# Two strips quantized in halves, a re-timed preparation queue and shared last combinations in a fused AdaLN/FFN kernel

## The chip, the cores and the metric

The kernel runs on one core of one Trainium2 chip. The metric is device time in microseconds (us) of one execution; the figure before is the median of three runs. Times inside an execution are counted from the start of the profiled span.

## What is computed

The reference, cut to what matters (`D = O = 2048`, 4096 tokens, everything f32):

```python
lora_delta = lora_B @ lora_A * 0.5
cb = codebook / max(abs(codebook))                  # 32 values, not sorted
normalized = (weight + lora_delta) / exp(scale_log) # groups of 128 columns
idx = searchsorted((cb[:-1] + cb[1:]) * 0.5, normalized, side='left')
quantized = cb[idx]
w = (quantized - normalized) + normalized
w_eff = w * exp(scale_log) + lora_delta
h = x @ w_eff.T
out = h @ W_base.T + b_base + 2 * mixed @ B_w.T     # mixed: router softmax over 8 rank-16 cores
return x + out
```

The kernel folds the two products: it computes `wc = W_base @ w_eff` (plus identity for the residual) once and then `x @ wc.T`.

## The kernel before

**Stage one: weights.** The weight matrix is handled in 16 strips of 128 columns (`[128, 16, 128]`, 2048 values for each partition). For each strip the quantizer walks the 31 thresholds in order. A level is one ACT instruction that writes a mask (`above`, L549, line of `raise_to`) and one DVE predicated copy that overwrites `a` with the level's value where the mask is set (L550). Four mask buffers let ACT run up to four levels ahead of DVE. The first levels of the *next* strip are made elsewhere: ACT makes the lowest level of each half in three passes (`scalar_level`: Relu L516, Sign L519, Identity L521; for level 3 of the first half the third pass is a Copy, L524), POOL makes two or three levels with a compare and an add each (`pool_levels`, L534 and L535) and adds level 3 (`last_level`, L539). So strips 1 to 5 have 27 full DVE levels, strips 6 to 15 have 27 and one half level.

After the last level, `straight_through` undoes and redoes the straight-through sum and multiplies by the scale (L572, L573, L574), on POOL in two halves, for the last strip on DVE in four quarters. Then TensorE multiplies the strip with four column blocks of `W_base`: `products(i, bs, c)` does quarter `c` of two blocks; the pair (2, 0) comes first, then (3, 1). Blocks 0 and 1 stay in SBUF, blocks 2 and 3 are streamed in 1 MB pieces (`wbp`) through three buffers. `low_rank` (L609) ends a block; `keep` copies it out of PSUM on ACT (L654) and stores it to `wc_dram` (L655). There are three PSUM buffers (`psum_m`) and five tiles for each strip (blocks 2, 0, the router part, 3, 1), so a new block waits for an older `keep`.

**Who sets the order.** Within this stage every engine runs its instructions in program order, and that order is written by hand: `behind(r, f, ...)` attaches a call to level `r`, and `quantize` emits those calls after the mask and copy of that level (I call this "hook r"). During strip `i` the hooks carry strip `i-1`'s products, strip `i+1`'s preparation (`delta` on TensorE, `scaled` on ACT, `normalize` on POOL, then the levels above) and, from strip 5 on, combinations of finished blocks.

**Combinations.** The second stage is a two-level Winograd-like product with seven by seven combined weights. `outer_w` and `inner_w` form these from `wc_dram` by adds and subtracts, and `put` stores them in `s_dram` (five DMAs for a pair of outer indices, three for a single one). For the first three groups this runs on POOL in the hooks (`made`). The last group (strips 12 to 15) can't be complete before the last strip is: outer index 1 needs strips 12 and 13 only (`first_fetch`, `first_make`, `first_put`); for blocks 0 and 2 the rest is `late_columns`, computed on DVE and put by DMAs issued from POOL; for blocks 1 and 3 it is done at the start of stage two (`last_fetch`, `last_outer`, `last_inner`, `last_put`). Tiles of stage two lie in memory that stage one used: `last_fetch(3)` fills a buffer that shares memory with `late`, so it waits until all of `late`'s puts have landed.

**Stage two.** 196 products `n` (L954), seven for each of 28 outer steps, with DVE, ACT and POOL combining the results; weights `s` are loaded from `s_dram` three products ahead on SP. DVE's part of the last combinations precedes its part of product 1 in DVE's program order (`u`, L1036).

Of the kernel before, what the change touches and what calls it, by code (L numbers as in the profile page):

```python
# [183 lines left out]
def adaln_ffn_kernel(  # L184
# [170 lines left out]
    def last_outer(b):  # L355
        outer_w(nc.vector, NK - 1, b)

    def last_inner(b, ms, z):
        inner_some(nc.vector, NK - 1, b, ms, z)

    def last_put(b, *sets):
        for ms in sets:
# [3 lines left out]
    with ExitStack() as sa:  # L366
# [145 lines left out]
        def scalar_level(i, f, r, part):  # L512
# [9 lines left out]
            elif part == 2:  # L522
                strips[i]["lx"] = mpool0.tile([P, NM // 2, P], F32, tag="lx", name=f"lx_{i}_{f}")
                nc.scalar.activation(strips[i]["lx"], sg, AF.Copy, scale=rise[:, r : r + 1])  # L524

        def half_step(i):
            return i - 1 in made

# [12 lines left out]
        def new_mask(i, r):  # L541
            return mpool.tile([P, F], F8, tag="above", name=f"above_{i}_{r}")

        def raise_to(i, r, above, f, n):
# [4 lines left out]
            nc.scalar.activation(above[:, c], q, AF.Relu, bias=neg_t[:, r : r + 1], scale=GAIN, saturate=False)  # L549
            nc.vector.copy_predicated(  # L550
                a, above[:, c].bitcast(U8), step[:, r : r + 1].to_broadcast([P, F // n])
            )

        def quantize(i, at):

            if half_step(i):
# [5 lines left out]
            assert not at, at  # L562

        def straight_through(i):
            last = i == NS - 1
            n = 4 if last else 2
            for h in range(n):
                m = ts(h, NM // n)
                w, a = strips[i]["w"][:, m, :], strips[i]["a"][:, m, :]
                sc = scale[:, strip[i], m].unsqueeze(2).to_broadcast([P, NM // n, P])  # L570
                v = nc.vector if last else nc.gpsimd
                v.tensor_tensor(a, a, w, ALU.subtract)  # L572
                v.tensor_tensor(a, a, w, ALU.add)  # L573
                v.tensor_tensor(a, a, sc, ALU.mult)  # L574
# [74 lines left out]

            nc.tensor.matmul(strips[i]["r"][:, P : P + RP], raw, stack, start=True, stop=True)  # L650

        def keep(i, b):
            out = spool.tile([P, 4, BC], F32, tag="out", name=f"out_{i}_{b}")
            nc.scalar.copy(out.rearrange("p q c -> p (q c)"), strips[i][b])  # L654
            (nc.scalar if i == NS - 1 else nc.sync).dma_start(wc_dram[i // 4][b][:, i % 4], out)  # L655

        def keep_router(i):
            nc.scalar.copy(rac[:, strip[i], :], strips[i]["r"][:, P : P + RP])
# [55 lines left out]
        def late_columns():  # L714

            t = big0.tile([P, NM, OQ], F32, tag="wb", name="late").rearrange("p m o -> p (m o)")
            for n, b in enumerate((0, 2)):
                f = t[:, 3584 * n : 3584 * n + 3584]
                columns(NK - 1, b, f[:, 0:2048], f[:, 2048:3584])
                fetch(NK - 1, b, range(3))  # L720
            for b in (0, 2):
                fetch(NK - 1, b, (3,))
            for b in (0, 2):
                if b == 0:
                    z = ypool.tile([P, 2048], F32, tag="up", name="late_z0")
                    z = (z[:, 0:1024], z[:, 1024:2048], t[:, 7168:8192])
                else:
                    more = ypool.tile([P, 1536], F32, tag="more", name="late_z1")
                    z = ypool.tile([P, 2048], F32, tag="up", name="late_z2")
                    z = (more[:, 0:1024], z[:, 0:1024], z[:, 1024:2048])  # L730
                last_outer(b)
                last_inner(b, (5, 6), z[0])
                last_inner(b, (2, 7), z[1])
                last_inner(b, (3,), z[2][:, 0:512])
                last_inner(b, (4,), z[2][:, 512:1024])
                last_put(b, (5, 6), (2, 7), (3,), (4,))


        made = {5: [(0, 0)], 6: [(0, 1)], 7: [(0, 2)], 8: [(0, 3)], 9: [(1, 0)], 10: [(1, 1)],
# [15 lines left out]
        for i in range(NS):  # L755
            at = {}

            def behind(r, f, *args):
                at.setdefault(r, []).append(lambda: f(*args))

            if i > 1:

                products(i - 2, (3, 1), NC - 1)
                route(i - 2, 0)
                behind(0, load_route, i - 2, 1)
                behind(2, keep, i - 2, 3)
                behind(3, keep, i - 2, 1)
            if i + 1 < NS:
                delta(i + 1, 0)
                if i > 0:  # L770
                    behind(1, load_w, i + 1, 2)
                behind(4, scaled, i + 1, 0)
                behind(4, normalize, i + 1, 0)
                behind(10, scaled, i + 1, 1)
                behind(10, normalize, i + 1, 1)
                for r, f, parts in ((0, 0, (11, 12, 13)), (NL - 1, 0, (14, 15, 18)), (0, 1, (19, 20, 21))):
                    for n, p in enumerate(parts):
                        behind(p, scalar_level, i + 1, f, r, n)
                behind(14, pool_levels, i + 1, 0)
                behind(19, last_level, i + 1, 0)  # L780
                behind(21, pool_levels, i + 1, 1)
            if i > 0:


                behind(9, load_route, i - 1, 0)
                if i == NS - 1:
                    behind(9, load_route, i - 1, 1)
                for c in range(2):
                    behind(2 + 3 * c, products, i - 1, (2, 0), c)
                if i + 1 < NS:  # L790
                    behind(7, delta, i + 1, 1)
                if i > 1:
                    behind(8, route, i - 2, 1)
                for c in range(2, NC):
                    behind(2 + 3 * c, products, i - 1, (2, 0), c)
# [5 lines left out]
                behind(19, router_sum, i - 1)  # L801
                behind(23, keep_router, i - 1)
                behind(18, router_parts, i - 1)
                if i + 2 < NS:
                    behind(20, load_la, i + 2)
            else:
                behind(3, nc.vector.reciprocal, rflat[:, NM:], flat[:, NM:])
                behind(7, delta, i + 1, 1)
                behind(22, lora_columns, 0)
                behind(24, lora_columns, 1)  # L810
                behind(25, lora_router)
            for n, (g, b) in enumerate(made.get(i, [])):
                step_of = (3, 5, 10, 13, 17, 23, 25) if len(made[i]) == 1 else (
                    (4, 6, 8, 9, 10, 12, 13) if n == 0 else (17, 19, 21, 22, 23, 24, 25)
                )
# [12 lines left out]

                behind((0, 14)[n], begin, g, b)
                r = step_of  # L830
                behind(r[0], outer_w, nc.gpsimd, g, b)
                behind(r[1], inner_pair, g, b, PAIRS[0])
                behind(r[1], inner_pair, g, b, PAIRS[1])
                behind(r[2], put, g, b, PAIRS[0])
                behind(r[3], put, g, b, PAIRS[1])
                behind(r[4], inner_pair, g, b, PAIRS[2])
                behind(r[4], inner_pair, g, b, PAIRS[3])
                behind(r[5], put, g, b, PAIRS[2])
                behind(r[6], put, g, b, PAIRS[3])
            quantize(i, at)  # L840
            straight_through(i)

        last = NS - 1
        products(last - 1, (3, 1), NC - 1)
# [10 lines left out]
        for bs in ((2, 0), (3, 1)):  # L855
            for c in range(NC):
                products(last, bs, c)
            if bs[0] == 2:
                multiply_router(last)
                router_parts(last)  # L860
            for b in bs:
                keep(last, b)
            if bs[0] == 2:
                router_sum(last)
                keep_router(last)
                late_columns()
        for h in range(2):
            route(last, h)
# [412 lines left out]
```

## Time and profile before

| | us |
|---|---|
| median of 3 runs | 2670.41 (2669.06 to 2674.28) |
| profiled execution | 2666.77 |
| its span | 2665.0 |
| TensorE busy | 2503.9 (94%) |
| DVE busy | 1549.0 (58%) |
| ACT busy | 1130.1 (42%) |
| POOL busy | 1367.2 (51%) |
| L550, DVE predicated copies | 1090.2 in 448 |
| L549, ACT masks | 872.4 in 448 |

The span falls into stage one (to about 1244.6, where the first product of stage two starts on TensorE) and stage two. Busy shares are means over both: DVE and ACT work nearly without a break in stage one and little in stage two, TensorE is nearly full in stage two. A row of the timeline gives the start, the length, the engine, the line, the operation with its tiles and shapes, how many instructions it merges, and in square brackets the idle time just before it with what ended it.

### The profile page before, as it was taken

To read this page: it belongs to the slowest core of one execution; us is meant where nothing else is said; L and a number is where in the kernel's file an instruction comes from. 1 tells how busy PE (TensorE), PEld (TensorE's weight loads), DVE (VectorE), ACT (ScalarE), POOL (GpSimd) and SP (SyncE) were. 2 spreads that over 40 slices of the span, in tenths; PEclk is the share of its full clock that TensorE was granted. 3 is DMA by queue.
4 is the path that set the end of the run, shared out by engine and by line. 5 is a ranking of instruction groups with operands and counts; after the bars stand their busy time and mean duration, and the time that the engine had idled before them with its cause. 6 is when DMAs were issued, how large, how long until landed. Compare 5 with 4: busy or idle time off the path is not lost.

```text
span 2665.0 us, 26423 instructions
## 1 busy us (share of the span) xinstructions
PE 2503.9 (94%) x10576; PEld 1704.1 (64%) x10576; DVE 1549.0 (58%) x990; ACT 1130.1 (42%) x796; POOL 1367.2 (51%) x783
## 2 busy tenths in 40 slices
PE   5499999999999999999999999999999999999999
PEld 2244444444444444345888888888888888888887
DVE  9999999999999999973433223242133332224221
ACT  7899999999999999930000000000000000000000
POOL 5777778889888888745313140042320323202224
PEclk9799999999999999999999999999999999999999
DMA  8255457776777777699844666536675455854554
GB/s 317 102 177 185 168 181 252 233 241 228 234 243 249 235 231 227 217 327 347 323 174 173 218 245 232 187 142 213 244 234 194 157 206 177 279 208 173 194 199 158
DMA packets 225979, 581.08 MB, mean 218 GB/s; under 512 B 20600, under 2 KB 121728, under 8 KB 182720
## 3 DMA queue, kind: packets, MB, share of 16 engines
q1 hardware_dynamic: 219296, 557.96, 61.1%
q0 software_dynamic: 4960, 14.95, 1.6%
q10 hardware_dynamic: 1600, 6.49, 0.7%
q8 instruction: 83, 1.36, 0.2%
q14 instruction: 40, 0.33, 0.0%
HBM read 477.62 MB, written 101.71 MB: 217 GB/s over the span
## 4 chain that ended last, share of the span: by engine, by line
PE 62%; ACT 17%; DVE 8%; POOL 7%; DMA 3%; issue 2%; SPq 0%; DVEq 0%; ACTq 0%; POOLq 0%
PE z L954 49%; ACT above L549 11%; PE m L621 10%; DVE a L550 7%; ACT sg L516 2%; ACT sg L519 2%; POOL a L572 1%; POOL a L573 1%; PE z L984 1%; ACT a L521 1%; POOL lv L534 1%; POOL a L574 1%; POOL a L535 1%; DMA xA<-in_xT 1%; DMA wc_dram<-out 1%
## 5 line engine op out<-in xcount | busy, mean ns | idle before, releaser
L550 DVE COPY_PREDICATED a<-above,step 128x2048 f32<-128x2048 uint8 (+1 forms) x448 | 1090.2, 2436 | 61.1 <-ACT above L549 19.3
L549 ACT ACTIVATE above<-w,neg_t 128x2048 fp8e5<-128x2048 f32 (+1 forms) x448 | 872.4, 1976 | 55.1 <-DVE a L550 44.5
L954 PE MATMUL z<-t,s 128*128 128x256 f32 x3584 | 791.4, 380 | 2.0 <-DVE u L1036 1.7
L954 PEld LDWEIGHTS z<-t,s 128*128 128x128 f32 x3584 | 677.5, 190 | 105.5 <-issue 13.2
L621 PE MATMUL m<-wbp,a 128*128 128x512 f32 x1024 | 502.1, 636 | 115.0 <-POOL a L574 101.0
L621 PE MATMUL m<-wb,a 128*128 128x512 f32 x1024 | 462.1, 594 | 4.4 <-ACT out L654 4.4
L621 PEld LDWEIGHTS m<-wbp,a 128*128 128x128 f32 x1024 | 202.6, 204 | 370.9 <-issue 239.7
L621 PEld LDWEIGHTS m<-wb,a 128*128 128x128 f32 x1024 | 194.5, 191 | 247.1 <-issue 242.4
L1034 ACT COPY m<-z 128x1024 f32<-128x1024 f32 x28 | 28.4, 1013 | 759.2 <-PE z L954 759.2
L1045 POOL TENSOR_TENSOR c<-u,m 128x1024 f32<-128x1024 f32 x16 | 50.1, 3130 | 443.8 <-DVE u L1042 422.4
L954 PE MATMUL z<-xA,s 128*128 128x256 f32 x1152 | 254.6, 379 | 0.0
L534 POOL TENSOR_SCALAR lv<-w,past,rise 128x1024 f32<-128x1024 f32 x65 | 245.9, 3783 | 3.7
L954 PEld LDWEIGHTS z<-xA,s 128*128 128x128 f32 x1152 | 218.8, 190 | 30.5 <-issue 0.8
L1045 POOL TENSOR_TENSOR M<-u,m 128x1024 f32<-128x1024 f32 x8 | 24.5, 3068 | 328.9 <-DVE u L1042 288.2
L954 PE MATMUL z<-xC,s 128*128 128x256 f32 x768 | 169.7, 379 | 0.0
L954 PE MATMUL z<-xB,s 128*128 128x256 f32 x768 | 169.7, 379 | 0.0
L535 POOL TENSOR_TENSOR a<-a,lv 128x1024 f32<-128x1024 f32 x65 | 154.3, 2374 | 27.1 <-ACT a L521 21.0
L1036 DVE TENSOR_TENSOR u<-z,m 128x1024 f32<-128x1024 f32 x28 | 34.3, 1224 | 218.5 <-issue 175.0
L1040 ACT COPY m<-z 128x1024 f32<-128x1024 f32 x28 | 28.3, 1011 | 308.8 <-PE z L954 308.8
L954 PEld LDWEIGHTS z<-xC,s 128*128 128x128 f32 x768 | 145.9, 190 | 19.8
L954 PEld LDWEIGHTS z<-xB,s 128*128 128x128 f32 x768 | 145.9, 190 | 19.8
L1042 DVE TENSOR_TENSOR u<-z,u 128x1024 f32<-128x1024 f32 x28 | 34.3, 1223 | 119.8 <-PE z L954 81.3
(213 smaller groups left out, 1958.0 us busy)
## 6 DMA issues: line engine op xcount, KB each, us to landing
s<-s_dram SPq DMA_DIRECT2D x196, 1024.0 KB, 4.9
wbp<-in_wbT SPq DMA_DIRECT2D x131, 1024.0 KB, 5.4
xs<-in_xT SPq DMA_DIRECT2D x64, 512.0 KB, 6.5
xA<-in_xT SPq DMA_DIRECT2D x24, 1024.0 KB, 9.4
s_dram<-z SPq DMA_DIRECT2D x84, 256.0 KB, 6.2
xB<-in_xT SPq DMA_DIRECT2D x16, 1024.0 KB, 10.4
outT<-M SPq DMA_DIRECT2D x16, 1024.0 KB, 12.5
w<-in_weight SPq DMA_DIRECT2D x30, 512.0 KB, 5.2
```

What stands on the lines that cost most here:

```text
L516: nc.scalar.activation(strips[i]["sg"], q, AF.Relu, bias=neg_t[:, r : r + 1], scale=GAIN)
L519: nc.scalar.activation(sg, sg, AF.Sign)
L534: v.tensor_scalar(lv, half(i, f, "w"), past[:, r : r + 1], rise[:, r : r + 1], ALU.is_gt, ALU.mult)
L535: v.tensor_tensor(a, a, lv, ALU.add)
L549: nc.scalar.activation(above[:, c], q, AF.Relu, bias=neg_t[:, r : r + 1], scale=GAIN, saturate=False)
L550: nc.vector.copy_predicated(a, above[:, c].bitcast(U8), step[:, r : r + 1].to_broadcast([P, F // n]))
L621: nc.tensor.matmul(ps, strips[i]["a"][:, CM * c + m, :], t[:, m, :], start=c == 0 and m == 0, stop=False)
L954: nc.tensor.matmul(z[:, c, :], s[:, k, ts(c, P)], rhs[:, k, :], start=not more and k == 0 and c % PER == 0, stop=k == NK - 1 and c % PER = ...
L1034: nc.scalar.copy(temp("m1", o), z["a"])
L1036: nc.vector.tensor_tensor(temp("u2", o), z["b"], state["m1", o], ALU.add)
L1042: nc.vector.tensor_tensor(temp("u3", o), z["d"], state["u2", o], ALU.add)
L1045: lambda d: nc.gpsimd.tensor_tensor(d, state["u3", o], state["m5", o], ALU.add),
```

## The change

- Strips 14 and 15 are quantized in two halves of the columns, one after the other: all levels of the first half (27 half levels), then all of the second (28). `straight_through` for the first half runs as soon as that half is done. A hook follows every second half level.
- For all other strips `straight_through` works on two quarters and then on the second half, where it worked on two halves. It stays on POOL but for the second half of the last strip, which is on DVE in two quarters.
- The second half of `delta`, the low-rank part of the next strip, moves from hook 7 (behind two quarters of the products) to hook 5 (behind one).
- `scaled`, `normalize`, the ACT passes, `pool_levels` and `last_level` get other hooks; the passes for the second half's lowest level come before those for level 3 of the first half.
- `keep` of blocks 2 and 0 moves from hooks 16 and 17 to hooks 14 and 15; `keep` of block 1 from 3 to 4; products from hooks 2, 5, 8, 11 to 4, 6, 8, 11.
- The combinations in the hooks get other places: two pairs early, the other two at hooks 24 and 25 with their puts at 25 and 26.
- For the last strip the two blocks of a pair are copied out of PSUM before anything is stored; the router's sum comes behind the first quarter of blocks 3 and 1.
- In `late_columns` both outer combinations come first on DVE; the inner ones of block 0 stay on DVE, those of block 2 go to POOL, between POOL's puts.

```diff
-        def straight_through(i):
-            last = i == NS - 1
-            n = 4 if last else 2
+        def halves(i, at):
+            n = 0
+            for f in range(2):
+                for k in range(T - NL + f):
+                    r = NL - f + k
+                    if n % 2 == 0:
+                        mask = new_mask(i, f"{f}{r}")
+                    raise_to(i, r, mask, f, 2, n % 2)
+                    n += 1
+                    if n % 2 == 0:
+                        for do in at.pop(n // 2 - 1, []):
+                            do()
+                if i == NS - 1 and f == 1:
+                    straight_through(i, f, nc.vector, 2)
+                else:
+                    straight_through(i, f, nc.gpsimd, 1 + f)
...
+            for f in range(2):
+                straight_through(i, f, nc.gpsimd, 2 - f)
...
-                behind(4, scaled, i + 1, 0)
-                behind(4, normalize, i + 1, 0)
-                behind(10, scaled, i + 1, 1)
-                behind(10, normalize, i + 1, 1)
-                for r, f, parts in ((0, 0, (11, 12, 13)), (NL - 1, 0, (14, 15, 18)), (0, 1, (19, 20, 21))):
+                behind(3, scaled, i + 1, 0)
+                behind(5, delta, i + 1, 1)
+                behind(7, scaled, i + 1, 1)
+                behind(5, normalize, i + 1, 0)
+                behind(9, normalize, i + 1, 1)
+                for r, f, parts in ((0, 0, (11, 12, 13)), (0, 1, (16, 17, 19)), (NL - 1, 0, (20, 21, 23))):
...
-                behind(16, keep, i - 1, 2)
-                behind(17, keep, i - 1, 0)
+                behind(14, keep, i - 1, 2)
+                behind(15, keep, i - 1, 0)
...
-                step_of = (3, 5, 10, 13, 17, 23, 25) if len(made[i]) == 1 else (
+                step_of = ((4, 8, 10), (4, 10, 12), (4, 24, 25), (4, 25, 26)) if len(made[i]) == 1 else (
...
+            for b in bs:
+                evacuate(last, b)
             if bs[0] == 2:
                 multiply_router(last)
                 router_parts(last)
             for b in bs:
-                keep(last, b)
+                store(last, b, nc.scalar)
...
+            last_inner(2, (5, 6), z[:, 0:1024], nc.gpsimd)
+            last_inner(2, (3,), z[:, 1024:1536], nc.gpsimd)
+            for b in (0, 2):
+                last_put(b, (5, 6))
+            last_put(2, (3,))
+            last_put(0, (2, 7), (3,), (4,))
+            z = ypool.tile([P, 2048], F32, tag="up", name="late_z2")
+            last_inner(2, (2, 7), z[:, 0:1024], nc.gpsimd)
+            last_inner(2, (4,), z[:, 1024:1536], nc.gpsimd)
+            last_put(2, (2, 7), (4,))
```

More of the change, by code (lines that the diff above doesn't have):

```diff
@@ L356, in last_outer, with last_inner @@
         outer_w(nc.vector, NK - 1, b)
-    def last_inner(b, ms, z):
-        inner_some(nc.vector, NK - 1, b, ms, z)
+    def last_inner(b, ms, z, v=nc.vector):
+        inner_some(v, NK - 1, b, ms, z)
     def last_put(b, *sets):
@@ L524, in scalar_level @@
                 nc.scalar.activation(strips[i]["lx"], sg, AF.Copy, scale=rise[:, r : r + 1])
+        HALVED = NS - 2
         def half_step(i):
@@ L542, in new_mask, with raise_to @@
             return mpool.tile([P, F], F8, tag="above", name=f"above_{i}_{r}")
-        def raise_to(i, r, above, f, n):
+        def raise_to(i, r, above, f, n, at=None):
             c = ts(f, F // n)
@@ L548, in raise_to @@
             a = strips[i]["a"].rearrange("p m i -> p (m i)")[:, c]
[L549 to L552, printed above, removed]
+            above = above[:, ts(f if at is None else at, F // n)]
+            nc.scalar.activation(above, q, AF.Relu, bias=neg_t[:, r : r + 1], scale=GAIN, saturate=False)
+            nc.vector.copy_predicated(a, above.bitcast(U8), step[:, r : r + 1].to_broadcast([P, F // n]))
         def quantize(i, at):
+            if i >= HALVED:
+                halves(i, at)
+                return
             if half_step(i):
@@ L561, in quantize, with straight_through @@
                     do()
-            assert not at, at
-        def straight_through(i):
-            last = i == NS - 1
-            n = 4 if last else 2
+            assert not at
+            for f in range(2):
[16 more added lines that the diff above has]
+                    straight_through(i, f, nc.gpsimd, 1 + f)
+            assert not at
+        def straight_through(i, f, v, n):
             for h in range(n):
-                m = ts(h, NM // n)
+                m = ts(n * f + h, NM // (2 * n))
                 w, a = strips[i]["w"][:, m, :], strips[i]["a"][:, m, :]
-                sc = scale[:, strip[i], m].unsqueeze(2).to_broadcast([P, NM // n, P])
-                v = nc.vector if last else nc.gpsimd
+                sc = scale[:, strip[i], m].unsqueeze(2).to_broadcast([P, NM // (2 * n), P])
                 v.tensor_tensor(a, a, w, ALU.subtract)
@@ L650, in router_sum, with evacuate, store, keep @@
             nc.tensor.matmul(strips[i]["r"][:, P : P + RP], raw, stack, start=True, stop=True)
-        def keep(i, b):
+        def evacuate(i, b):
             out = spool.tile([P, 4, BC], F32, tag="out", name=f"out_{i}_{b}")
             nc.scalar.copy(out.rearrange("p q c -> p (q c)"), strips[i][b])
-            (nc.scalar if i == NS - 1 else nc.sync).dma_start(wc_dram[i // 4][b][:, i % 4], out)
+            strips[i]["out", b] = out
+        def store(i, b, q=nc.sync):
+            q.dma_start(wc_dram[i // 4][b][:, i % 4], strips[i]["out", b])
+        def keep(i, b):
+            evacuate(i, b)
+            store(i, b)
         def keep_router(i):
@@ L723, in late_columns @@
             for b in (0, 2):
[L724 to L730, printed above, removed]
-                last_outer(b)
[L732 to L736, printed above, removed]
+                last_outer(b)
+            z = ypool.tile([P, 2048], F32, tag="up", name="late_z0")
+            last_inner(0, (5, 6), z[:, 0:1024])
+            last_inner(0, (2, 7), z[:, 1024:2048])
+            last_inner(0, (3,), t[:, 7168:7680])
+            last_inner(0, (4,), t[:, 7680:8192])
+            z = ypool.tile([P, 1536], F32, tag="more", name="late_z1")
+            last_inner(2, (5, 6), z[:, 0:1024], nc.gpsimd)
[8 more added lines that the diff above has]
+            last_put(2, (2, 7), (4,))
         made = {5: [(0, 0)], 6: [(0, 1)], 7: [(0, 2)], 8: [(0, 3)], 9: [(1, 0)], 10: [(1, 1)],
@@ L766, in adaln_ffn_kernel @@
                 behind(2, keep, i - 2, 3)
-                behind(3, keep, i - 2, 1)
+                behind(4, keep, i - 2, 1)
             if i + 1 < NS:
@@ L771, in adaln_ffn_kernel @@
                     behind(1, load_w, i + 1, 2)
-                behind(4, scaled, i + 1, 0)
-                behind(4, normalize, i + 1, 0)
-                behind(10, scaled, i + 1, 1)
-                behind(10, normalize, i + 1, 1)
-                for r, f, parts in ((0, 0, (11, 12, 13)), (NL - 1, 0, (14, 15, 18)), (0, 1, (19, 20, 21))):
+                behind(3, scaled, i + 1, 0)
[4 more added lines that the diff above has]
+                for r, f, parts in ((0, 0, (11, 12, 13)), (0, 1, (16, 17, 19)), (NL - 1, 0, (20, 21, 23))):
                     for n, p in enumerate(parts):
                         behind(p, scalar_level, i + 1, f, r, n)
-                behind(14, pool_levels, i + 1, 0)
-                behind(19, last_level, i + 1, 0)
-                behind(21, pool_levels, i + 1, 1)
+                behind(13, pool_levels, i + 1, 0)
+                behind(19, pool_levels, i + 1, 1)
+                behind(23, last_level, i + 1, 0)
             if i > 0:
@@ L788, in adaln_ffn_kernel @@
                 for c in range(2):
-                    behind(2 + 3 * c, products, i - 1, (2, 0), c)
-                if i + 1 < NS:
-                    behind(7, delta, i + 1, 1)
+                    behind((4, 6, 8, 11)[c], products, i - 1, (2, 0), c)
                 if i > 1:
@@ L794, in adaln_ffn_kernel @@
                 for c in range(2, NC):
-                    behind(2 + 3 * c, products, i - 1, (2, 0), c)
+                    behind((4, 6, 8, 11)[c], products, i - 1, (2, 0), c)
                 behind(13, multiply_router, i - 1)
-                behind(16, keep, i - 1, 2)
-                behind(17, keep, i - 1, 0)
+                behind(14, keep, i - 1, 2)
+                behind(15, keep, i - 1, 0)
                 for c in range(NC - 1):
                     behind((17, 20, 22)[c], products, i - 1, (3, 1), c)
-                behind(19, router_sum, i - 1)
-                behind(23, keep_router, i - 1)
+                behind(20, router_sum, i - 1)
+                behind(24, keep_router, i - 1)
                 behind(18, router_parts, i - 1)
@@ L807, in adaln_ffn_kernel @@
                 behind(3, nc.vector.reciprocal, rflat[:, NM:], flat[:, NM:])
-                behind(7, delta, i + 1, 1)
                 behind(22, lora_columns, 0)
@@ L812, in adaln_ffn_kernel @@
             for n, (g, b) in enumerate(made.get(i, [])):
[L813 to L814 removed]
+                step_of = ((4, 8, 10), (4, 10, 12), (4, 24, 25), (4, 25, 26)) if len(made[i]) == 1 else (
+                    ((4, 6, 8), (6, 6, 9), (10, 10, 12), (10, 10, 13)) if n == 0 else
+                    ((17, 19, 21), (19, 19, 22), (23, 23, 24), (23, 23, 25))
                 )
@@ L830, in adaln_ffn_kernel @@
                 r = step_of
[L831 to L839, printed above, removed]
+                behind(r[0][0], outer_w, nc.gpsimd, g, b)
+                for k, pair in enumerate(PAIRS):
+                    behind(r[k][1] if k else r[0][1], inner_pair, g, b, pair)
+                    behind(r[k][2], put, g, b, pair)
             quantize(i, at)
-            straight_through(i)
         last = NS - 1
@@ L857, in adaln_ffn_kernel @@
                 products(last, bs, c)
+                if bs[0] == 3 and c == 0:
+                    router_sum(last)
+                    keep_router(last)
+            for b in bs:
+                evacuate(last, b)
             if bs[0] == 2:
@@ L861, in adaln_ffn_kernel @@
             for b in bs:
-                keep(last, b)
+                store(last, b, nc.scalar)
             if bs[0] == 2:
-                router_sum(last)
-                keep_router(last)
                 late_columns()
```

## The prediction

> **What bounds the kernel now.** I read the page first, then the timeline of one strip engine by engine, then the chain of waits and the timeline where stage one hands over to stage two.
>
> ```profile
> PE 2503.9 (94%) x10576; PEld 1704.1 (64%) x10576; DVE 1549.0 (58%) x990; ACT 1130.1 (42%) x796; POOL 1367.2 (51%) x783
> ...
> L550 DVE COPY_PREDICATED a<-above,step 128x2048 f32<-128x2048 uint8 (+1 forms) x448 | 1090.2, 2436 | 61.1 <-ACT above L549 19.3
> L549 ACT ACTIVATE above<-w,neg_t 128x2048 fp8e5<-128x2048 f32 (+1 forms) x448 | 872.4, 1976 | 55.1 <-DVE a L550 44.5
> ```
>
> TensorE's 94% belongs to stage two. In stage one the bound is the row of predicated copies: 1090 us busy and 61 idle in about 1150. A full level takes DVE 2.47 us plus a gap of 0.10, so 2.57; a strip with 27 levels and a half one needs 70.8. The strips come every 71.6 (1029.84 to 1101.41). The difference is DVE waiting for a mask, 19.3 us in all, of which 49 ordinary gaps of 0.1 make 5. So all hook shuffling can win at most some 14 us.
>
> ```profile
> 1054.61 1.02 ACT L502 ACTIVATE a<-d 128x1024 f32<-128x1024 f32 x1 [3.34 <-PE d L410]
> ...
> 1088.78 70.49 DVE L550 COPY_PREDICATED a<-above,step 128x2048 f32<-128x2048 uint8 x28 [0.55 <-ACT above L549]
> ...
> 1106.50 1.90 POOL L574 TENSOR_TENSOR a<-a,scale 128x1024 f32<-128x1024 f32 x1
> ...
> 1108.45 6.34 PE L621 MATMUL m<-wbp,a 128*128 128x512 f32 x8 [5.60 <-POOL a L574]
> ```
>
> ACT loses its lead at hook 10, where it waits 3.34 us for the low-rank part; then five passes in a row (1.04, 0.94, 1.13 us) on top of a 1.90 us mask overrun DVE's 2.57. TensorE idles 5.6 us at each strip's start for POOL's first half and then runs slowly: 6.34 us for eight matmuls that otherwise take 3.60.
>
> ```profile
> L550 DVE COPY_PREDICATED a<-above,step 128x1024 f32<-128x1024 uint8 x14 | 18.3, 1317 | 0.2
> ```
>
> This is the half level: 1.33 us inside a strip, 1.43 with its gap.
>
> ```profile
> 1191.19 23.45 DMA xA<-in_xT
> ...
> 1215.74 5.40 PE L621 MATMUL m<-wb,a 128*128 128x512 f32 x8 [4.43 <-ACT out L654]
> ...
> 1226.21 2.62 DVE L320 TENSOR_TENSOR late<-late 128x512 f32<-128x512 f32 x4 [44.27 <-DMA late<-wc_dram]
> ...
> 1253.65 0.55 POOL L353 DMA_DIRECT2D s_dram<-late x1
> 1261.37 2.13 POOL L310 DMA_DIRECT2D last<-wc_dram x3 [7.16 <-DMA s_dram<-late]
> ...
> 1274.31 2.62 DVE L320 TENSOR_TENSOR last<-last 128x512 f32<-128x512 f32 x4 [9.12 <-DMA last<-wc_dram]
> ...
> 1288.53 7.17 PE L954 MATMUL z<-t,s 128*128 128x256 f32 x32 [1.71 <-DVE u L1036]
> ```
>
> This is the handover chain. The last strip's store sits behind xA's landing; then load, DVE combination, POOL's puts, the fetch for block 3 (only when all puts have landed), DVE again, and product 6 of TensorE waits 1.71 us for DVE. So what sets the end is not where stage two starts (1244.58) but when DVE gets through, and POOL is in that chain.
>
> **The change, part by part.** Times are from the start s of a strip, "before" from the trace.
>
> *Strips 1 to 13.* The first POOL quarter ends at 0.18 + 1.36 + 1.36 + 1.03 = 3.9 (512 columns take POOL 1.28 at L320, 1.36 with the gap; the multiply is taken as 1.03, somewhat over half of 1.90). Before, it was a half, at 7.0. TensorE thus starts 3.05 us earlier and ends blocks 2 and 0 at 37.65 where it was 40.7. `delta`'s second half now ends at about 14.7, so the 3.34 us stall shrinks to about 1 and is made up by hook 11. But the keep of block 2 stands at hook 14, two levels (5.14 us) earlier. ACT's greatest lead is three levels less a mask, 5.65, about 4.7 at hook 14: it arrives at 32.7 and waits 5 us for TensorE. The copy (0.47) and the next mask (2.0) end at 40.12, just when DVE wants level 15 (1.43 + 15 x 2.57 = 40.0). With the lead gone, the passes at 16, 17, 20 and 21 cost DVE 0.17 + 0.27 + 0.30 + 0.27; with 0.1 at level 15 that is 1.1, and about 0.1 of other gaps. Measured before: 0.8 on average in strips 6 to 13. So 0.4 more a strip, 3.4 in eight. In strips 1 to 5, which lack the half level, the same count gives 8.4 against 8.6. Together +3.2. One us of TensorE's arrival moves this by nearly one us a strip, so the term lies between -8 and +8.
> SP and POOL: the late puts at hooks 25 and 26 hold SP until POOL is through at about 69. Behind them stand a `wbp` piece that is needed 22 us into the next strip, the fetch for `up` (needed at 14) and the weight load (waits for POOL until 12.4 anyway): nothing if POOL keeps time, up to 2 us a strip if it doesn't. POOL's sum is 14.1 + 5.1 + 8.7 + 5.6 + 25 + 2.4 + 4.7 = 65.6 of 71.6.
>
> *Strips 14 and 15.* 55 half levels at 1.43 make 78.6 instead of 70.8: DVE ends 15.6 later in all. A rule of the Trainium skill speaks against this too: "VectorE: DVE Perf Modes", section on the TRN2 errata, says SBUF operations pay a fixed time per instruction, about 150 cycles as measured there. At 0.96 GHz that estimate is 0.156 us, so 27.5 more instructions would cost 4.3 a strip. The row says 2 x 1.43 - 2.57 = 0.29 each, 8 a strip, since each copy also waits for a mask; I take the row. What is it worth for TensorE? Products of 14 could start 5 us sooner, but block 0 needs the PSUM tile of the previous block 3, whose keep is at hook 2 of strip 15: ACT gets there at s14 + 79.9 (four mask buffers). The keep at hook 14 then holds blocks 3 and 1 until 112.8, the one behind the last mask holds strip 15's block 0 until 148.9, and quarter 2 needs DVE's end plus 2.5 = 159.5. Blocks 2 and 0 of strip 15 end at s14 + 175.3. Before: 1205.1 - 1029.84 = 175.3. Gain of halving: 0, with -4 to +6.
>
> *Handover.* Copying both blocks before storing removes TensorE's 4.43 + 0.35 us and the router's detour: stage two starts 5.5 earlier. xA's load comes at s14 + 161 as before (160.7; it waits for DVE's last subtract-add), but the x loads before it start about 4 us earlier, so fewer bytes are queued; I put the late combination's start t0 at s14 + 190 where it was 196.4 (bounds 188 and 196.4).
> Then POOL. Before, 32 puts of 0.72 ran from t0 + 1 to t0 + 28. Now POOL starts at t0 + 5.3 and has, besides, two pairs of 2.8 and two singles of 1.85, 9.3 us, all in one queue: last put at about t0 + 38.5. The landing (7.2 before, taken 6.5) gives the fetch at t0 + 45, where it was 35.2. Its data took 12.9 with stage two's loads around it; in the now quieter place I take 10. DVE resumes at t0 + 55, and needs 14.2 as before: t0 + 69.2 against 62.3. That is s14 + 259.2 against 258.7: +0.5, with -4 to +7. DVE's own saving, 5.4 us in `late_columns`, is worth nothing: it waits for the fetch.
> TensorE reaches product 6 at s14 + 251.4 and so idles 8 us. "TensorE: Matmul & The Clock Gate", Part 1, says that after an idle window of about 3.4 us the array runs at half rate for about as long, an estimate of 1.7 us lost. In the trace 4.5 to 5.6 us of idle cost 2.7 (6.34 against 3.60), the 1.71 us at product 6 nothing visible. I take 2.6; if the idle time is under 3 us it is 0.
>
> Sum: 3.2 + 0 + 0.5 + 2.6 = +6.3 on the profiled execution's 2666.77 (span 2665.0 and 1.8 around it), so 2673.1. The median of the runs shown is 3.6 above that execution: 2676.7, given as 2677. A measurement of this kernel can tell about 0.2%, 5.3 us, from no change.
>
> **Rivals.**
> *ACT keeps its lead (faster).* If TensorE ends blocks 2 and 0 only 1 us earlier than I count, all passes fit and each strip loses its 0.8: -8 in stage one. With t0 at s14 + 188 and a fetch of 8 us the handover adds -3.5 + 2.6. Sum -9, about 2662. For: the passes are spread better and the 3.34 us stall goes. Against: the keep at hook 14. Chance 0.20.
> *The handover doesn't come earlier (slower still).* The store waits for xA as before, t0 stays at s14 + 196.4, POOL's extra 7 us are paid in full, 265.6 against 258.7: +6.9 + 2.6 + 3.2 = +12.7, about 2683; to 2690 if DVE's longer halves also show. It decides from xA landing later than s14 + 183. Chance 0.18.
> *Terms cancel (no change).* No cold start and 0 in the strips leaves +0.5, about 2671. Chance 0.12.
> *My forecast*, 2670 to 2684 alone: 0.50, of which 0.12 lies within 0.2%.
> Slower 0.38 + 0.18 = 0.56, same 0.12 + 0.12 = 0.24, faster 0.20. For the range I leave out the lower half of the faster case and the top of the slower one: 2662 to 2688.
>
> **What would show it.** Right: ACT idle about 5 us at hook 14 for TensorE in each strip, with a small idle at hook 7; strips every 72.0; strips 14 and 15 of about 78.6 with half levels of 1.33; the fetch of block 3 about 45 us after the first late DVE combination; an idle of 4 to 12 us before product 6, then slow matmuls. Wrong: strips at 71.0 or less; product 6 without a wait; the start of stage two not earlier against strip 14's start; POOL idle gone at the end of strips, with TensorE starting later than 4 us.

## The result and the profile after

The changed kernel takes 2679.49 us (median of 7 runs, 2679.01 to 2684.2) where before takes 2670.41: ratio 1.0034, with a 95% interval of 1.0023 to 1.0045, so about 9 us slower. Its profiled execution took 2679.18, with a span of 2677.4. The profiled pair is 12.4 apart in span, more than the medians: before's profiled execution (2666.77) lies 3.6 below its median, after's 0.3 below.

From the page of after, engines and groups of instructions:

```profile
PE 2502.5 (93%) x10576; PEld 1703.2 (64%) x10576; DVE 1555.5 (58%) x1022; ACT 1136.6 (42%) x850; POOL 1391.9 (52%) x847
...
L554 DVE COPY_PREDICATED a<-above,step 128x2048 f32<-128x2048 uint8 (+1 forms) x502 | 1098.9, 2193 | 67.2 <-ACT above L553 20.6
L553 ACT ACTIVATE above<-w,neg_t 128x2048 fp8e5<-128x2048 f32 (+1 forms) x502 | 878.6, 1791 | 38.0 <-DVE a L554 28.3
```

TensorE's work is unchanged. In the DVE row the wait for masks hardly moved (20.6 where it was 19.3). In the ACT row the number behind the last bar tells more: ACT waits for DVE only when it is as far ahead as the four mask buffers allow. That wait fell from 44.5 to 28.3 us, so ACT was ahead less often. The half levels, in the groups by shape:

```profile
L554 DVE COPY_PREDICATED a<-above,step 128x1024 f32<-128x1024 uint8 x122 | 159.7, 1313 | 11.1
```

The timeline shows the loss in two places. The rows below give start, length, engine, line, operation, and in brackets the idle time before; first strip 10 in the middle of stage one, then the handover:

```profile
749.89 5.68 PE L646 MATMUL m<-wbp,a 128*128 128x512 f32 x8 [5.83 <-POOL a L599]
760.37 1.02 ACT L502 ACTIVATE a<-d 128x1024 f32<-128x1024 f32 x1 [0.43 <-PE d L410]
783.40 0.58 ACT L679 COPY out<-m 128x512 f32<-128x512 f32 x1 [4.65 <-PE m L634]
...
1222.98 2.62 DVE L320 TENSOR_TENSOR late<-late 128x512 f32<-128x512 f32 x4 [30.67 <-DMA late<-wc_dram]
1229.05 1.09 POOL L329 TENSOR_TENSOR late_z<-late 128x256 f32<-128x256 f32 x1 [10.60 <-DVE late L320]
1230.61 0.94 DVE L329 TENSOR_TENSOR late_z<-late 128x256 f32<-128x256 f32 x1
...
1256.98 0.72 POOL L329 TENSOR_TENSOR late_z<-late 128x256 f32<-128x256 f32 x1 [1.78 <-DMA s<-s_dram]
...
1266.71 0.55 POOL L353 DMA_DIRECT2D s_dram<-late  x1
1276.44 1.23 DVE L965 TENSOR_TENSOR t<-t,xA 128x1024 f32<-128x1024 f32 x1 [34.80 <-DMA s_dram<-late_z]
1277.14 2.15 POOL L310 DMA_DIRECT2D last<-wc_dram  x3 [9.88 <-DMA s_dram<-late]
1284.31 2.62 DVE L320 TENSOR_TENSOR last<-last 128x512 f32<-128x512 f32 x4 [2.64 <-DMA last<-wc_dram]
...
1298.51 9.60 PE L987 MATMUL z<-t,s 128*128 128x256 f32 x32 [15.79 <-DVE u L1069]
```

In stage one the stall for the low-rank part (3.1 to 3.5 us before, in strips 6 to 13) is 0.43 in strip 10, but ACT now stands 4.65 us at hook 14, where the `keep` of block 2 waits for TensorE. In the handover, DVE has its data 3.2 us earlier than before (1222.98 against 1226.21), POOL's last put is out 44.3 us after that, and the fetch for block 3 follows only when everything has landed. DVE, held by the same puts, stands idle for 34.80 us, and product 6 of TensorE waits 15.79 us instead of 1.71.

The span difference in three terms, with s14 the start of strip 14 and product 6 counted from it:

| | before | after | difference |
|---|---|---|---|
| s14 | 1029.84 | 1032.45 | +2.6 |
| product 6 starts, from s14 | 258.7 | 266.1 | +7.4 |
| product 6 lasts | 7.17 | 9.60 | +2.4 |
| sum | | | +12.4 |

### The profile page after: what moved, and what is told of

Its sections match the earlier page's. It is cut to its first block, busy times and chain, and to the rows that moved or that the text cites. A ratio compares the mean times of both kernels' runs of the same rounds, so it can differ in the third digit from the quotient of the medians.

```text
span 2677.4 us, 26622 instructions
## 1 busy us (share of the span) xinstructions
PE 2502.5 (93%) x10576; PEld 1703.2 (64%) x10576; DVE 1555.5 (58%) x1022; ACT 1136.6 (42%) x850; POOL 1391.9 (52%) x847
## 4 chain that ended last, share of the span: by engine, by line
PE 70%; ACT 13%; DVE 10%; POOL 3%; DMA 2%; issue 1%; SPq 0%; DVEq 0%; ACTq 0%; POOLq 0%
PE z L987 49%; PE m L646 17%; DVE a L554 9%; ACT above L553 9%; PE z L1017 1%; ACT sg L516 1%; ACT sg L519 1%; POOL a L597 1%; POOL a L598 1%; PE m L634 1%; PE d L410 1%; ACT a L521 1%; POOL a L599 1%; DMA wc_dram<-out 0%; PE acc L706 0%
## 5 line engine op out<-in xcount | busy, mean ns | idle before, releaser
L554 DVE COPY_PREDICATED a<-above,step 128x2048 f32<-128x2048 uint8 (+1 forms) x502 | 1098.9, 2193 | 67.2 <-ACT above L553 20.6
L553 ACT ACTIVATE above<-w,neg_t 128x2048 fp8e5<-128x2048 f32 (+1 forms) x502 | 878.6, 1791 | 38.0 <-DVE a L554 28.3
L1073 ACT COPY m<-z 128x1024 f32<-128x1024 f32 x28 | 28.3, 1011 | 308.5 <-PE z L987 308.5
```

The lines of the kernel that those rows point to most:

```text
L553: nc.scalar.activation(above, q, AF.Relu, bias=neg_t[:, r : r + 1], scale=GAIN, saturate=False)
L554: nc.vector.copy_predicated(a, above.bitcast(U8), step[:, r : r + 1].to_broadcast([P, F // n]))
L1073: nc.scalar.copy(temp("m5", o), z["c"])
```

## The experiments

My theory after the result: the loss is the new `late_columns`, above all POOL's longer queue, and the strips hide a gain that the `keep` at hook 14 takes back. The rivals: the loss comes from the halves of strips 14 and 15, or from the earlier passes in the strips. Ratios are to the kernel before, in runs beside it on the same chip, with 95% intervals.

### 1. The change with the former `late_columns`

```diff
-            last_inner(2, (5, 6), z[:, 0:1024], nc.gpsimd)
-            last_inner(2, (3,), z[:, 1024:1536], nc.gpsimd)
...
+                last_inner(b, (5, 6), z[0])
+                last_inner(b, (2, 7), z[1])
+                last_inner(b, (3,), z[2][:, 0:512])
+                last_inner(b, (4,), z[2][:, 512:1024])
+                last_put(b, (5, 6), (2, 7), (3,), (4,))
```

> The changed kernel with one part undone: late_columns is the former one (all combinations on DVE, block by block, puts as before). My theory (POOL's queue in the handover sets product 6): POOL's last put of `late` at about 28 us after the first late combination instead of 44, the fetch for block 3 at 35 instead of 54, product 6 of stage two within 4 us of its natural place, no slow matmuls; the time falls by 12 to 17 us against the changed kernel, to 2662 to 2668, below the kernel before. Rival (the handover wait comes from loads and memory, not from POOL's queue): product 6 still waits 8 us or more, and the time stays within 5 us of the changed kernel.

2671.14 us, ratio 0.9998 (0.9990 to 1.0007): no change against before, 8.4 less than after. The direction is as expected, the size is short of it. From its timeline:

```profile
1267.29 2.12 POOL L310 DMA_DIRECT2D last<-wc_dram  x3 [5.53 <-DMA s_dram<-late]
1278.26 7.07 PE L982 MATMUL z<-xA,s 128*128 128x256 f32 x32
1292.68 3.78 PE L982 MATMUL z<-t,s 128*128 128x256 f32 x8 [7.35 <-DVE u L1064]
```

The fetch comes 39.0 us after the first late combination (1228.32) where after has 54.2. But product 6 still waits 7.35 and starts slowly (its 32 matmuls take 9.93), where under 4 and no slow matmuls were expected. TensorE reaches it early: the earlier start of stage two has turned into a wait. Here `late` also came later than in after (s14 + 194.2 against 190.5), which took part of the gain.

### 2. Before, with the new `late_columns` alone

The same edit the other way round, on the kernel before.

> The kernel before with only the shared late_columns put in. My theory: it costs here what it costs in the changed kernel or a little more, since stage two starts later here: product 6 waits 13 to 16 us instead of 1.7 and starts slowly (2.4 us): +13 to +17 us, 2683 to 2688. Rival (the sharing is harmless by itself and hurts only with the earlier stage two): +0 to +4 us.

2682.98, ratio 1.0042 (1.0027 to 1.0057): 10.7 slower, somewhat less than expected. Its timeline:

```profile
1266.73 0.55 POOL L353 DMA_DIRECT2D s_dram<-late  x1
1276.34 2.16 POOL L310 DMA_DIRECT2D last<-wc_dram  x3 [9.07 <-DMA s_dram<-late]
...
1302.04 9.62 PE L959 MATMUL z<-t,s 128*128 128x256 f32 x32 [12.63 <-DVE u L1041]
```

With nothing else changed, the fetch moves from 35.2 to 48.3 us after the first late combination, and product 6 pays 12.63 and a slow start. Taken out (run 1) or put in (run 2), this edit is worth 8 to 11 us: the whole loss.

### 3. Run 1, with `keep` of blocks 2 and 0 back at hooks 16 and 17

```diff
-                behind(14, keep, i - 1, 2)
-                behind(15, keep, i - 1, 0)
+                behind(16, keep, i - 1, 2)
+                behind(17, keep, i - 1, 0)
```

> As x1_late_before, and the keeps of blocks 2 and 0 put back from hooks 14 and 15 to 16 and 17, nothing else. My theory (ACT loses its lead by waiting 4.65 us for TensorE at hook 14): the wait shrinks to under 1 us, ACT keeps a lead of 3 us or more, DVE's idle times go, strips 6 to 13 come every 70.9 to 71.1 us instead of 71.7 and strips 3 to 5 every 69.7 to 70.2 instead of 71.8; strip 14 starts 10 to 14 us earlier and the time falls by as much against x1_late_before. Rival (POOL, which has 3 us of slack, or TensorE sets the strips next): strips fall by 0.3 us or less each, the time by under 4 us.

2658.3, ratio 0.9948 (0.9934 to 0.9963): 12.8 less than run 1, as expected. ACT in strip 10:

```profile
748.33 1.02 ACT L502 ACTIVATE a<-d 128x1024 f32<-128x1024 f32 x1 [1.87 <-PE d L410]
...
771.36 0.59 ACT L679 COPY out<-m 128x512 f32<-128x512 f32 x1 [0.52 <-PE m L634]
```

And its row of masks:

```profile
L553 ACT ACTIVATE above<-w,neg_t 128x2048 fp8e5<-128x2048 f32 (+1 forms) x502 | 882.7, 1790 | 71.7 <-DVE a L554 60.4
```

The `keep` waits 0.52 instead of 4.65, and ACT is held back by DVE for 60.4 us where it was 28.3: it keeps its lead. Between the copies of strips 1 to 13 DVE idles 38.0 us, in run 1 55.0; the 359 ordinary gaps of 0.1 make 36 of both. Strips 6 to 13 come every 70.9 to 71.3, and strip 14 starts 16.9 us earlier than in run 1 (10 to 14 were expected).

### 4. Run 1 without the halves

```diff
-        HALVED = NS - 2
+        HALVED = NS
```

The last strip's second half of `straight_through` goes to DVE as in the change.

> As x1_late_before, but strips 14 and 15 are quantized in whole levels again, the last strip's straight-through sum on DVE in four quarters. My theory (halving is worth nothing: blocks 2 and 0 of the last strip end 174 to 175 us after strip 14's start either way): within 3 us of x1_late_before; strips 14 and 15 of 70.8 us instead of 77.6. Rival 1 (halving lets TensorE start earlier): slower by 4 to 8 us. Rival 2 (halving's 13.6 us of longer DVE work shows): faster by 4 us or more.

2671.52, ratio 1.0001 (0.9992 to 1.0010): the same as run 1. Strips 14 and 15 take 71.5 and 71.2 instead of 77.6 each, and yet blocks 2 and 0 of the last strip end at s14 + 175.3, against 177.2 in run 1 and 174.4 in after. Ends of DVE's levels that are over 12 us apart give ends within 2 us on TensorE.

### 5. After, with block 2's combinations on DVE but in the new order

```diff
-            last_inner(2, (5, 6), z[:, 0:1024], nc.gpsimd)
-            last_inner(2, (3,), z[:, 1024:1536], nc.gpsimd)
+            last_inner(2, (5, 6), z[:, 0:1024])
+            last_inner(2, (3,), z[:, 1024:1536])
...
-            last_inner(2, (2, 7), z[:, 0:1024], nc.gpsimd)
-            last_inner(2, (4,), z[:, 1024:1536], nc.gpsimd)
+            last_inner(2, (2, 7), z[:, 0:1024])
+            last_inner(2, (4,), z[:, 1024:1536])
```

> The changed kernel, block 2's inner combinations on DVE again, but in the new order of late_columns (both outer ones first, the puts of outer index 2, 7 and 4 of block 2 last). It separates POOL's arithmetic from the order. My theory (arithmetic in POOL's put queue, and POOL and DVE slowing each other while both combine): last put of `late` at about 34 us after the first late combination instead of 44, product 6 waits 6 to 9 us instead of 15.8; time 2669 to 2674, about that of x1_late_before. Rival (the order alone does it, since the single buffer for the last two combinations is refilled only after a landing): last put still at 40 us or later, time within 3 us of the changed kernel.

2677.76, ratio 1.0023 (1.0015 to 1.0031). Missed: the time, 1.7 us under after, is the one that the rival gave. In the trace the last put does come sooner, 36.9 us after the first combination against 44.3 (the rival had 40 or more), but a new wait took its place. The 15 runs spread from 2672.04 to 2683.92, and the profiled one, 2674.01, is among the lowest. Its timeline:

```profile
1252.14 0.42 DVE L329 TENSOR_TENSOR late_z<-late 128x256 f32<-128x256 f32 x1 [13.94 <-DMA s_dram<-late]
...
1257.20 8.06 PE L987 MATMUL z<-t,s 128*128 128x256 f32 x29 [10.48 <-issue]
```

DVE must wait 13.94 us for the buffer of block 2's later combinations, which is free only when block 0's puts from it have landed, and what makes product 1's input (`t`, L965) stands behind that in DVE's program order. Product 1 waits 10.48, product 6 no longer. Against run 1 the last put is 3.5 us later for the order of the puts; POOL's arithmetic added the other 7.4. So the order and POOL's arithmetic can be told apart in the traces; by the time, the order alone costs nearly as much as both.

### 6. Run 3 without the halves

> As x3_keep16, and strips 14 and 15 in whole levels as in x4_no_halves. My theory (halving is worth nothing to TensorE and costs DVE 13.6 us that only just hide): blocks 2 and 0 of the last strip end 175 us after strip 14's start instead of 179, product 6 comes 0 to 4 us earlier, time 2654 to 2659. Rival (halving gains once stage one runs faster): slower than x3_keep16 by 4 us or more.

2653.93, ratio 0.9932 (0.9917 to 0.9947): the fastest kernel here, 17.8 us under before and 25.6 under after. Run 3's interval overlaps, so it is not resolved whether leaving out the halves brings something; a gain from having them shows in neither pair (1 and 4, 3 and 6). This kernel differs from run 4 by the two `keep` calls alone, and takes 17.6 us less.

### 7. and 9. Before, with `delta`'s second half alone moved

```diff
-                    behind(7, delta, i + 1, 1)
+                    behind(3, delta, i + 1, 1)
```

> The kernel before with one edit: the second half of delta stands at hook 3, behind one quarter of the products, instead of hook 7, behind two. My theory (the 3.34 us stall of ACT at hook 10 was what cost the strips of the kernel before): no stall at hook 10, ACT waits about 2 us for TensorE at hook 16 with lead to spare; strips 6 to 13 every 70.9 to 71.1 us instead of 71.7, strips 3 to 5 about 70.5; the time falls by 7 to 10 us, to 2661 to 2665. Rival (the passes in a row cost it, not the stall): strips fall by 0.3 us or less, the time by under 4 us.

2730.5, ratio 1.0213. At hook 3 the second half's low-rank part is made before ACT has read the first half's (hook 4), and there is one PSUM buffer for both, so the edit changes part of the computation and its waits: the time says nothing on the question. Run 9 asks it with hook 4 (`behind(4, delta, i + 1, 1)`).

> The kernel before with one edit: the second half of delta at hook 4 instead of 7, still behind the first half's scaled, on TensorE behind one quarter of the products instead of two. My theory (ACT's 3.34 us stall at hook 10 was what cost the strips of the kernel before): no stall at hook 10, ACT waits about 2 us for TensorE at hook 16 with lead to spare; strips 6 to 13 every 70.9 to 71.3 us instead of 71.7, strips 3 to 5 about 70.5 instead of 71.5; the time falls by 7 to 10 us, to 2662 to 2665. Rival (the passes in a row cost it, not the stall): strips fall by 0.3 us or less, the time by under 4 us.

2658.67, ratio 0.9952 (0.9937 to 0.9967): 12.9 faster for one number, more than the 7 to 10 expected. Between the profiled executions it is 8.0; the rest is before's low profiled execution. Strip 10, first the second half's row in before, then three rows of this run, where the wait of 3.48 is gone:

```profile
768.23 1.02 ACT L502 ACTIVATE a<-d 128x1024 f32<-128x1024 f32 x1 [3.48 <-PE d L410]
...
744.62 1.02 ACT L502 ACTIVATE a<-d 128x1024 f32<-128x1024 f32 x1
759.16 1.00 ACT L502 ACTIVATE a<-d 128x1024 f32<-128x1024 f32 x1
778.31 0.58 ACT L654 COPY out<-m 128x512 f32<-128x512 f32 x1 [1.68 <-PE m L609]
```

s14 falls from 1029.84 to 1022.21, which is nearly the whole difference of the pair; product 6 waits 1.70 as in before. The first quarter that lets TensorE start earlier isn't needed for this.

### 8. Run 3, with block 2's 16 puts issued by ACT

```diff
-                last_put(b, (5, 6), (2, 7), (3,), (4,))
+                if b == 0:
+                    last_put(b, (5, 6), (2, 7), (3,), (4,))
...
+                for ms in ((5, 6), (2, 7), (3,), (4,)):
+                    put(NK - 1, 2, ms, nc.scalar)
```

> As x3_keep16, with block 2's sixteen puts of late_columns issued from ACT's DMA queue behind the last stores instead of from POOL's. My theory (POOL's queue of 32 puts at 0.72 us each is what the fetch of block 3 waits for): the puts are all issued 25 us after the first late combination instead of 31, the fetch goes out at 31 to 33 instead of 36.7, product 6 waits under 3 us instead of 7.4 and does not start slowly; 5 to 9 us less than x3_keep16, 2649 to 2653. Rival (landing, not issuing, or ACT's own work behind the puts sets it): within 3 us of x3_keep16.

2664.76, ratio 0.9973 (0.9962 to 0.9985), 6.5 slower than run 3, so that theory and rival both missed. In its timeline (ACTq is ACT's issue of DMAs):

```profile
1230.08 1.37 ACTq L351 DMA_DIRECT2D s_dram<-late  x1
...
1244.99 1.07 ACT L902 COPY accs<-acc 128x512 f32<-128x512 f32 x2 [17.33 <-DMA s_dram<-late_z]
1246.12 6.11 PE L986 MATMUL z<-t,s 128*128 128x256 f32 x17 [10.60 <-ACT accs L902]
```

A put holds ACT for up to 1.37 us, the copies behind them come 17 us late, and product 1 waits 10.60. The fetch for block 3 is no earlier: 39.5 us after the first late combination (36.7 in run 3). POOL's half of the puts is over after 16.9, but ACT begins its half only at 13.7 and ends it at 30.6, no sooner than POOL ended all 32 in run 3 (30.7). The run therefore doesn't show what puts issued earlier would be worth.

### 10. Before, with only "copy both blocks, then store" and the router's sum moved

```diff
+            for b in bs:
+                evacuate(last, b)
...
-                keep(last, b)
+                store(last, b, nc.scalar)
```

> The kernel before with one part of the change: the last strip's two blocks are copied out of PSUM before either is stored, and the router's sum comes a quarter later. My theory (product 6 of stage two waits for the handover chain, not for TensorE): TensorE's 4.43 us idle goes and stage two starts 4 to 6 us earlier, but the first late combination and the fetch of block 3 stay within 2 us of their places, product 6 waits 5 to 8 us instead of 1.7 and starts slowly; time within -2 to +3 us of before. Rival (stage two's start sets the end): faster by 4 to 6 us.

2671.57, ratio 1.0001 (0.9992 to 1.0009). From its timeline:

```profile
1239.17 6.09 PE L964 MATMUL z<-xA,s 128*128 128x256 f32 x27
...
1289.93 10.07 PE L964 MATMUL z<-t,s 128*128 128x256 f32 x32 [3.38 <-DVE u L1046]
```

Stage two starts 5.4 us before that of the kernel before (1244.58), and `late` comes no earlier (s14 + 197.1 against 196.4), so TensorE waits longer: 3.76 at product 1 and 3.38 at product 6 (5 to 8 expected there). The gain is lost whole. The fetch for block 3 was expected to keep its place and didn't: it comes 40.2 us after the first late combination, 35.2 in before. SP's loads for stage two go out about 7 us earlier, and POOL idles 9.3 us between the first and the last of its 32 puts where it idled 4.3.

### 11. After, with only the two `keep` calls at hooks 16 and 17

The edit of run 3, on after.

> The changed kernel with only the keeps of blocks 2 and 0 back at hooks 16 and 17. My theory: stage one gains what it gained in x3_keep16 (strip 14 about 15 us earlier), the handover costs what it cost in the changed kernel; time 12 to 15 us below the changed kernel, 2665 to 2668, so this one hook decides the sign of the whole change. Rival (the handover eats the gain): within 5 us of the changed kernel.

2667.83, ratio 0.9985 (0.9978 to 0.9991), 11.7 less than after: two numbers turn the change from slower to faster than before. s14 is 1016.57 where it was 1032.45. Product 6 still waits 16.11 us for DVE:

```profile
1286.42 9.06 PE L987 MATMUL z<-t,s 128*128 128x256 f32 x32 [16.11 <-DVE u L1069]
```

### 12. Run 6, with block 0's 16 puts issued by SP

```diff
-                last_put(b, (5, 6), (2, 7), (3,), (4,))
+                for ms in ((5, 6), (2, 7), (3,), (4,)):
+                    put(NK - 1, b, ms, nc.sync if b == 0 else nc.gpsimd)
```

> As x6_keep16_no_halves, with block 0's sixteen puts of late_columns issued from SP's queue, ahead of the first three loads of s, and only block 2's from POOL's. My theory (the fetch of block 3 waits for POOL's 32 puts): POOL's last put of `late` at 22 to 24 us after the first late combination instead of 28.5, the fetch at 29 to 32 instead of 36, product 6 is ready 4 to 7 us earlier; but the first loads of s are issued about 10 us later, so stage two starts 3 to 5 us later; together 0 to 4 us faster than x6_keep16_no_halves, 2650 to 2654. Rival (SP's queue held back costs more than POOL's saves): slower by 2 us or more.

2663.4, ratio 0.9969 (0.9954 to 0.9983), 9.5 slower than run 6, as the rival said; the profiled execution, 2657.4, is 4.1 above that of run 6. From its timeline:

```profile
1232.45 2.93 PE L986 MATMUL z<-xA,s 128*128 128x256 f32 x6 [8.76 <-DMA s<-s_dram]
...
1233.51 0.78 POOL L352 DMA_DIRECT2D s_dram<-late_z  x1 [1.78 <-DMA s_dram<-late_z]
1234.78 0.55 POOL L353 DMA_DIRECT2D s_dram<-late  x1 [0.49 <-DMA s<-s_dram]
1243.06 2.84 POOL L310 DMA_DIRECT2D last<-wc_dram  x4 [7.72 <-DMA last<-wc_dram]
```

The first weights of stage two stand behind the puts in SP's queue, and the fetch again comes no sooner (35.6 us after the first late combination; 36.2 in run 6). SP's half of the puts is out after 14.0, yet POOL's 16 last until 27.9, where its 32 were over at 28.5 in run 6: POOL stands 5.1 us between them for earlier transfers to land, and then 7.7 before the fetch. So where POOL has no arithmetic in its queue, the landings are the limit, and not POOL's issuing.

## Why the prediction was right, and where its steps failed

- **The direction and the three-term sum.** Slower, by strips, a later product 6 and a slow start there. The terms were forecast at +3.2, +0.5 and +2.6; they measured +2.6, +7.4 and +2.4. Their sum is twice the forecast, 12.4 against 6.3. The medians are only 9.1 apart, since before's profiled execution was a low one and after's was not; so far the nearness of 2677 to 2679.49 is luck.
- **`keep` at hook 14.** The stall was forecast at 5 us and measured 4.65, with the small one at the low-rank part 0.43 (forecast 1) and TensorE's first quarter 4.0 us into the strip (forecast 3.9). Three pairs that differ by the two `keep` calls alone show what they cost: 12.8 us (runs 1 and 3), 17.6 (4 and 6) and 11.7 (after and 11). What was not seen is how large the gain is that they cancel: s14 is 12.6 earlier than before in run 3 and 13.3 in run 11, close under the 14 us that the first view gave as the most that hooks could win.
- **The strips one by one** failed: strips 6 to 13 were forecast at +3.4 and measured +0.5, strips 1 to 5 at -0.2 and +1.7, and strip 0 added 0.3. The errors cancel in the total, which is luck. The step that failed is the count of DVE's small waits at 1.1 a strip against 0.8 before. Strips 6 to 13 in fact come nearly as before, every 71.7 on average (71.6 before; 72.0 was forecast), and DVE idles 28.5 us between their copies, 28.7 before. In strips 1 to 5 it idles 24.6 where it was 22.7: in strips 2 to 5 the one wait behind hook 14 is 1.2 to 1.8 us, where 0.1 was counted.
- **The halves** are worth nothing, as worked out: 77.6 a strip (forecast 78.6), blocks 2 and 0 of the last strip at s14 + 174.4 (forecast 175.3), and runs 4 and 6. Of the two prices weighed for a half copy, the row's 0.29 us was a little nearer than the 0.156 estimated from the Trainium skill's page "VectorE: DVE Perf Modes": (77.6 - 71.3) / 27.5 is 0.23.
- **The start of the handover** was right: `late` at s14 + 190.5 (forecast 190), stage two at s14 + 206.7 (forecast 209.2). Run 10 shows that the second of these by itself is worth nothing, as the reading of the chain of waits said.
- **POOL's queue in the handover** is the mis-sized term. Forecast was a last put 38.5 us after the first late combination; it was out at 44.3. POOL began 0.8 later. Its waits in the middle of the puts come to about 2.8 for earlier transfers and 1.78 for the one buffer that block 0's combinations and block 2's later ones share. DVE and POOL also combined more slowly than their rows in before (last section). The landing took 9.88 (forecast 6.5), so the fetch came at 54.2 (forecast 45). The fetch itself was quicker, 7.2 (forecast 10), but not for a quieter place: the DMA engines' busy share during it is 0.94, and 1.04 during before's fetch of 12.9. Put together: 0.5 + 9.2 - 2.8 = +6.9, which is the gap between s14 + 259.2 and 266.1. Product 6 so waits 15.79 us, outside the 4 to 12 forecast. It starts about where the rival "slower still" put it (s14 + 265.6), but by another way: that rival had `late` at s14 + 196.4, and it came at 190.5.
- **The slow start** at product 6: forecast 2.6, measured 2.43. The reading behind it took the upper end: in before, idle times of 4.4 to 5.6 us cost 1.8 to 2.7 (for 4.43 the prediction's own row shows 5.40 against 3.60).

What stays open: why the waits for landings take so long in the handover. Run 12 shows that POOL's issuing is not the limit where its queue holds only puts, but no run showed which transfers are in the way. The traces give a hint that no run tests. In stretches of 5 us from 1213 to 1283 the DMA engines of after are busy 0.94 of the time or more, but for one: 0.31 from 1233 to 1238, when POOL combines and its puts only begin (the first goes out 12.35 us after the first late combination, in before after 0.99). The puts that come later share the engines with loads of 1 MB for stage two, and in run 10, where these loads come earlier, the puts are slower. A version with a second buffer for block 2's combinations on POOL was not tried.

## What to carry to other kernels

An engine with an in-order queue and a lead of a few buffers loses that lead at the first instruction whose producer isn't done. One hook number can be worth more than a rewrite (run 9: one number, -12.9; run 11: two numbers, -11.7), so compare each moved wait with the time at which its producer ends. Before you start a stage earlier, or shorten one engine's work in it, follow the chain that ends last: here it ran through POOL's puts and their landing, and the new `late_columns`, with arithmetic in that queue and another order of the puts, lengthened it although DVE had less to do.

## What the runs showed of the hardware

- **DVE and POOL slow each other while both combine.** Groups by shape of after, then of before, two-input f32 operations of 256 columns; the third number is the mean in ns:

```profile
L329 POOL TENSOR_TENSOR late_z<-late 128x256 f32<-128x256 f32 x2 | 1.8, 904 | 12.4 <-DVE late L320 10.6 <-DMA s<-s_dram 1.8
L329 DVE TENSOR_TENSOR late_z<-late 128x256 f32<-128x256 f32 x2 | 1.6, 808 | 0.0
```

```profile
L329 DVE TENSOR_TENSOR late_z<-late 128x256 f32<-128x256 f32 x4 | 1.7, 420 | 2.3 <-DMA s_dram<-late 2.3
```

  DVE needs 808 ns instead of 420, and is back at 410 for the one operation that it does after POOL has finished. POOL's mean of 904 mixes 1.09 us beside DVE with 0.72 alone (the rows at 1229.05 and 1256.98 above).
- **The slow start after an idle TensorE.** At product 6, 32 matmuls take 7.17 us after 1.70 us of idle, and 10.07 after 3.38, 8.71 after 5.46, 9.60 after 15.79: a loss of 1.5 to 2.9 that doesn't grow with the idle time. It is a lower granted clock: in run 10 the clock is 0.50 for the first 5.9 us of product 6 and then 1.00, in after 0.74 on average over the 9.60, in before 1.00 over the 7.17. The length of the idle time alone doesn't decide: 3.43 us before product 1 of run 4 cost nothing (7.15, clock 1.00), 3.38 in run 10 cost 2.9. The row of run 6 that the 8.71 is from:

```profile
1273.43 8.71 PE L985 MATMUL z<-t,s 128*128 128x256 f32 x32 [5.46 <-DVE u L1067]
```

- **Taking half of the puts from POOL's queue did not bring the transfer behind them forward** (39.5 us after the first late combination in run 8 against 36.7, 35.6 in run 12 against 36.2), and ACT, when it issues a put, stands up to 1.37 us for it (run 8).
